# Where the operand rooms of a two-layer graph kernel lie modulo 128 bytes

## The chip, the core and the metric

The kernel runs on one core of one Trainium2 chip. The metric is the device time of one execution in microseconds. The kernel before was run three times: 1642.21, 1644.04 and 1644.42 us, so its median is 1644.04 us. One further execution was profiled: its own time was 1642.81 us, and the profile's span, from the first instruction to the last, is 1641.0 us.

Engine names below are those of the profile: PE multiplies, PEld loads the weights that a product needs, DVE is the vector engine, ACT the scalar engine, POOL the general one, and SP issues most DMAs.

## The reference, cut to what matters

Sixty-four samples of 256 rows by 512 columns go through two layers, and all samples share one 256 by 256 adjacency matrix of zeros and ones.

```
h   = relu(layernorm(x))
q, k, v = h @ Wq.T, h @ Wk.T, h @ Wv.T
rel = adj.T * (q @ k.T)
rel = rel / norm(rel, axis=2)
x   = x + rel @ v
h   = relu(layernorm(x))
x   = x + (adj @ h) @ weight + bias
```

## The kernel before, in words

**Arithmetic.** Wq and Wk are multiplied once, at the start, into one matrix `m`, so that `q @ k.T` becomes `h m h.T`. Most operands are split into three rounded parts, u, l and s ("upper", "lower" and a third one), and a product is then three sums: u by u, l by l and s by s. `three` (L329) builds such a product. The u and l sums are issued first. ACT then rescales the PSUM bank in place (L321, in `unit`), and the s sums are added behind the next unit's u and l sums.

**Tiling.** Two samples make a pair, and there are 32 pairs. For each pair PE runs six stages:

| Stage | Moving operand (right) | Loaded as weights (left) | Columns | Products |
|---|---|---|---|---|
| `g_stage` | `h_u`, `h_l`, `hs` | `m_u`, `m_l`, `m_s` | 512 | 48 |
| `v_stage` | `wv_u`, `wv_l`, `wv_s` | `h_u`, `h_l`, `hs` | 512 | 48 |
| `scores` | `h_u`, `h_l`, `hs` | `gy_u`, `gy_l`, `gy_s` | 256 | 48 |
| `attend` | `v_low`, `late_parts` | `rel_u`, `rel_l`, `rel_s_parts` | 512 | 24 |
| `gather` | `adjt_r` | `v_low`, `late_parts` | 256 | 32 |
| `mix` | `w_u`, `w_l`, `w_s` | `gy_u`, `gy_l`, `gy_s` | 512 | 48 |

All of them are issued by one line, L213. PE loads the weights of a product while the product before it streams. Layer 2 of a pair (`gather`, `mix`) runs in the middle of layer 1 of the next pair.

**Order.** `Plan` (L31) collects every operation with a cost and what it reads and writes, works out a due time for each, and emits one fixed order per engine. Every engine then works through its own list in that order and waits where an input is late.

**The work between the products.** The names that matter later, by line:

- L223, L224, L226 (`split_right_ps`): ACT writes the u part of a finished bank, DVE the s part and then the l part. For `g_stage` these are `gy_u`, `gy_s` and `gy_l`, for block columns e = 0 to 3.
- L232 to L234 (`split_left_ps`): the same for the results of `gather`.
- L250 to L260 (`norm`): DVE statistics, one square root on ACT (L256), then the reciprocal and `nb` on DVE.
- L264 (`relu`): ACT writes the normalized rows, for layer 2 into `rel_s_raw`. L477 (ACT) and L478 (DVE) split them into the parts that `gather` loads. L481 (POOL) adds the bias.
- L286 (`h_turn`): DVE transposes the next pair's rows into the rooms `h_s0` and `h_s1`, whose tiles are named `ht` and then `hs`. It has to wait until `v_stage` has read the old `hs` for the last time. L300, L302 and L295 make the three parts.
- L396 (DVE) and L400 (ACT): the masked scores and their norms. L415: 16 small DMAs on SP move the scores. L421 (DVE) transposes them, and L431 to L433 split them.
- L457 (DVE) adds the result of `attend` to x, L519 that of `mix`.

**Where the rooms lie.** `room` (L142) makes a tile in a pool with a single buffer. Rooms follow one another in the order in which they are first made, at a grain of 32 bytes per partition, and a room with a known tag reuses that tag's place. From the first room to `ident`, every size is a multiple of 128 bytes. Then come `ones`, `low_max`, `low_any`, the statistics and the norms, 928 bytes together, which is 7 times 128 plus 32. With the first room's place called 0, the program's addresses modulo 128 are:

| Place | Rooms |
|---|---|
| 0 | `m`, `wv`, `w` (all parts), `h_u`, `h_l`, `gy_u`, `gy_l` (the tags of `wq_sb`, `wk_sb`), `rel_u` (the tag of `adj_low`), `v_low` |
| 32 | `gy_s`, `rel_l`, `adjt_r`, `h_s0` and `h_s1`, `late_parts`, `rel_s` |

Offsets inside these rooms are multiples of 128 bytes throughout. So the distance, modulo 128, from a moving operand to the weights loaded while it streams is:

| Stage | u sums | l sums | s sums |
|---|---|---|---|
| `g_stage` | 0 | 0 | 96 |
| `v_stage`, `mix` | 0 | 0 | 32 |
| `scores` | 0 | 0 | 0 |
| `attend` | 0 or 96 | 0 or 32 | 0 or 32 |
| `gather` | 0, and 96 where `v_low` is loaded | | |

Where one group of sums ends and the next begins, the distance is that from the last moving operand of the one to the first weights of the other.

Of the kernel before, what the change touches and what calls it, by code (L numbers as in the profile page):

```python
# [10 lines left out]
F32R = mybir.dt.float32r  # L11
# [101 lines left out]
def kernel(  # L113
# [13 lines left out]
    B, N, D = x.shape  # L127
    DC = D // P
    NC = N // P
    NB = 2  # L130
    TC = NB * NC
    T = NB * N
# [9 lines left out]
    def room(name, *shape, dtype=F32, tag=None):  # L142
        return pool.tile([P, *shape], dtype, name=name, tag=tag or name)

    def parts_room(name, *shape, tag=None):
        return [room(f"{name}_{k}", *shape, dtype=F32R, tag=f"{tag or name}_{k}") for k in "uls"]
# [1 line left out]
    bank = [ps_m.tile([P, 512], F32, name=f"bank{n}") for n in range(8)]  # L148
    fresh = room("fresh", TC, D)
    ring = [room(f"x_ring{n}", TC, D) for n in range(2)]  # L150
    m_p, wv_p, w_p = (parts_room(w, DC, D) for w in ("m", "wv", "w"))
    h = [room(f"h_{k}", DC, T, dtype=F32R) for k in "ul"]
    ht, h_s = [None, None], [None, None]

    def hp(k, d):
        return h[k][:, d] if k < 2 else h_s[d // 2][:, d % 2]
    wq_sb, wk_sb = room("wq_sb", DC, D, tag="gy_u"), room("wk_sb", DC, D, tag="gy_l")
    adj_low = room("adj_low", 2, D, tag="rel_u")
    v_low = room("v_low", 4, D, dtype=F32R)
    blocks = room("blocks", TC, DC, P)  # L160
# [34 lines left out]
        for j in range(2)  # L195
    ]
    norms = [room(f"rn{n}", NB, NC) for n in range(2)]

    V, A, G, SP = nc.vector, nc.scalar, nc.gpsimd, nc.sync
    count = {"bank": 0}  # L200
# [38 lines left out]
    def load(plan, i, src=None, name="fresh"):  # L239

        dst = fresh if name == "fresh" else ring[i % 2]
        plan.add("SP", 0.65, lambda: SP.dma_start(out=dst, in_=xs[i]), [], keys(name, TC), lands=5.5)
# [24 lines left out]
    def h_rows(plan, i, src=fresh, name="fresh"):  # L267
        relu, needs = norm(plan, i, 0, src, name)
        for c in range(TC):
            plan.add("ACT", 0.72, lambda c=c: relu(h_rel[:, c, :], c),  # L270
                     [(name, c), *needs], [("h_rel", c)])

    def h_place(plan):
        hv = h_rel.rearrange("p c (d e) -> p c d e", e=P)

        for j in range(P // S):
            for k in range(P // S):
                plan.add("SP", 0.65, lambda j=j, k=k: SP.dma_start(  # L278
                    out=blocks[ts(j, S), :, :, ts(k, S)], in_=hv[ts(k, S), :, :, ts(j, S)]),
                    keys("h_rel", TC), [("blocks", j, k)], lands=2.3)  # L280
# [9 lines left out]
    def h_parts(plan):  # L290
        u, l = h

        def third(k, at):
            h_s[k] = room(f"hs{k}", 2, T, dtype=F32R, tag=f"h_s{k}")
            V.scalar_tensor_tensor(h_s[k], f(l[:, at]), CROSS, f(u[:, at]), op0=ALU.mult, op1=ALU.subtract)  # L295
        for k in range(2):
            d = 2 * k
            at = slice(d, d + 2)
            ku, kl, ks = ([(f"h_{q}", d), (f"h_{q}", d + 1)] for q in "uls")
            plan.add("ACT", 0.96, lambda k=k, at=at: A.activation(  # L300
                u[:, at], ht[k], AF.Copy, scale=NEAR), ks, ku)
            plan.add("DVE", 1.14, lambda k=k, at=at: V.tensor_sub(  # L302
                l[:, at], ht[k], f(u[:, at])), [*ks, *ku], kl)
            plan.add("DVE", 1.14, lambda k=k, at=at: third(k, at), [*ku, *kl], ks)
# [3 lines left out]
    def finish(plan):  # L308
        while waiting:
            waiting.pop(0)()  # L310
# [50 lines left out]
    def g_stage(plan, i):  # L361
        for e in range(DC):
            first, second = three(
                lambda k, d, e=e: m_p[k][:, d, ts(e, P)], hp,
                named("m_u", "m_l", "m_s"), h_named, MM)
            unit(plan, first, second, lambda ps, key, e=e: split_right_ps(
                plan, ps, key, [lambda at, q=q: q[:, at, :] for q in gy],
                gy_both(e), e))
# [182 lines left out]
    def before_pairs():  # L551
        A.activation(low_max, ones, AF.Sqrt)
        for _ in range(8):
            mm(bank[7][:, :P], warm, warm, True)
        V.tensor_single_scalar(low, adj_low[:, 0].bitcast(I32), 0xFFF, op=ALU.bitwise_and)
        V.tensor_reduce(low_max, low, axis=mybir.AxisListType.X, op=ALU.max)
        mm(bank[7][0:1, 0:1], low_max, ones, True)
        V.tensor_copy(low_any, bank[7][0:1, 0:1])
        for m in range(NC):
            for n in range(NC):  # L560
                nc.tensor.transpose(bank[6][:, ts(m * NC + n, P)], adj_sb[:, n, ts(m, P)], ident)
        for e in range(DC):
            for i in range(DC):
                mm(bank[i], wq_sb[:, e, ts(i, P)], wk_sb[:, e, :], e == 0)
        plan = Plan()
        h_rows(plan, 0, ring[0], "x0")
        plan.run()
        plan = Plan()
        for i in range(DC):
            split_right_ps(plan, bank[i], ("bank", i), [lambda at, q=q: q[:, at, :] for q in m_p],  # L570
                           [[("m_u", i)], [("m_l", i)], [("m_s", i)]], i)
        plan.run()

    with tc.manual_schedule(engines=in_order):
        before_pairs()
    gy = parts_room("gy", DC, T)
    rel_p = [room(f"rel_{k}", NB, NC, NC, P, dtype=F32R) for k in "ul"]
    adjt = []
    inexact = nc.values_load(low_any[0:1, 0:1], min_val=0, max_val=P * 0xFFF)
# [3 lines left out]
    def first_turn(plan):  # L583
        for d in range(DC):
            ps, key = next_bank()

            def go(ps=ps, d=d):
                for c in range(TC):
                    nc.tensor.transpose(ps[:, ts(c, P)], h_rel[:, c, ts(d, P)], ident)

            def copy(ps=ps, k=d // 2, d=d % 2):
                if not d:
                    ht[k] = room(f"ht{k}", 2, T, tag=f"h_s{k}")
                A.copy(ht[k][:, d], ps)
            plan.add("PE", 0.44, go, keys("h_rel", TC), [key])
            plan.add("ACT", 0.49, copy, [key, *([("h_s", d - 1)] if d % 2 else [])], [("h_s", d)])

    def turn_wv(plan):
        for d in range(DC):
            ps, key = next_bank()  # L600

            def go(ps=ps, d=d):
                for e in range(DC):
                    nc.tensor.transpose(ps[:, ts(e, P)], wv_sb[:, e, ts(d, P)], ident)
            plan.add("PE", 0.44, go, placed_all, [key])
            split_right_ps(plan, ps, key, [lambda at, q=q: q[:, at, :] for q in wv_p],
                           [[("wv_u", d)], [("wv_l", d)], [("wv_s", d)]], d)
# [6 lines left out]
    def pairs(exact):  # L614
        count["bank"] = 4
        waiting.clear()
        rooms.clear()
        plan = Plan()
        adjt[:] = [room("adjt_r", NC, N, dtype=F32R, tag="adjt") if exact else room("adjt", NC, N)]
        plan.add("ACT", 0.49, lambda: A.copy(adjt[0].rearrange("p m n -> p (m n)"), bank[6]), [("bank", 6)], ["adjt"])  # L620
        first_turn(plan)
        h_parts(plan)
        turn_wv(plan)
        g_stage(plan, 0)
        h_rows(plan, 1)
        h_place(plan)
        load(plan, 2)
        v_stage(plan, 0, exact, (0,))
        scores(plan, 0)
        v_stage(plan, 0, exact, (1, 2, 3))  # L630
        split_w(plan)
        finish(plan)
        turn_scores(plan, 0)
        h_turn(plan)
        h_parts(plan)
        attend(plan, 0, exact)
        for i in range(1, NP):
            load(plan, i, name=f"x{i % 2}")
            if i + 1 < NP:
                h_rows(plan, i + 1)  # L640
                h_place(plan)
            if i + 2 < NP:
                load(plan, i + 2)
            g_stage(plan, i)
            v_stage(plan, i, exact, (0,))
            v_stage(plan, i, exact, (1,), hold=True)
            scores(plan, i)
            gather(plan, i - 1, exact)
            while held:
                held.pop(0)()  # L650
            v_stage(plan, i, exact, (2, 3))
            turn_scores(plan, i)
            if i + 1 < NP:
                waiting.append(lambda: (h_turn(plan), h_parts(plan)))
                mix(plan, i - 1)
                attend(plan, i, exact)
            else:
                mix(plan, i - 1, (0, 1))
                attend(plan, i, exact)
                mix(plan, i - 1, (2, 3))  # L660
                finish(plan)
            store(plan, i - 1)
        gather(plan, NP - 1, exact)
        mix(plan, NP - 1)
        finish(plan)
        store(plan, NP - 1)
        with tc.manual_schedule(engines=in_order):
            plan.run()
# [33 lines left out]
```

## Time and profile before

| What | Value |
|---|---|
| Median of three runs | 1644.04 us |
| Profiled execution, own time | 1642.81 us |
| Its span | 1641.0 us |
| One pair in the steady middle (pairs 2 to 30) | 48.70 us |
| DVE busy in such a pair | 44.1 us |
| ACT busy in such a pair | 29.5 us |
| POOL busy in such a pair | 6.8 us |
| PE products in such a pair | 168 of 512 columns, 80 of 256 |
| First pair; last pair with the tail | 58.5 us; 77.5 us |

Times inside a pair are microseconds from the start of the span. A matmul record's duration contains a pipelined part: in this trace it is the distance to the next matmul's start plus about 163 ns. Distances between starts are therefore what PE's pace is read from, and the mean durations of two groups differ as their distances do.

### The profile page before, as it was taken

Reading aid. Unit: us, or ns where it says so; the run is one execution under the profiler, and the core shown is the slowest. Engines: PE = TensorE matmul, PEld = TensorE weight load, DVE = VectorE, ACT = ScalarE, POOL = GpSimd, SP = SyncE. Lnnn points to the kernel's source line nnn. Section 1 sums busy time; section 2 is a strip of 40 time slices with the busy share of each in tenths; the row PEclk is TensorE's granted clock in tenths of the full one; section 3 lists DMA queues with packets and bytes.
Section 4 is the critical chain, followed back from the end, with each engine's and each line's share of the span. In section 5 each row is a group of like instructions: output and inputs, shape, how many; then the busy total and the mean of one; then the engine's idle time right before and its main releaser. Section 6 shows DMA issues by size and latency. Waiting matters only on the chain.

```text
span 1641.0 us, 22555 instructions
## 1 busy us (share of the span) xinstructions
PE 1594.9 (97%) x8022; PEld 1338.1 (82%) x8022; DVE 1432.7 (87%) x2423; ACT 958.1 (58%) x1811; POOL 217.5 (13%) x168
## 2 busy tenths in 40 slices
PE   7699999999999999999999999999999999999997
PEld 4578888888888888888888888888888888888875
DVE  4789999889989889989889999888998988998874
ACT  3455656656655656565655565665665665666553
POOL 0011101111101111100111110111110111110011
PEclk9899999999999999999999999999999999999998
DMA  4324432444433343433344442344343334343111
GB/s 167 90 58 110 116 63 75 107 113 107 115 73 86 87 115 106 114 93 78 79 112 109 110 116 62 78 107 112 107 116 68 83 95 115 106 114 90 39 39 54
DMA packets 445882, 155.22 MB, mean 95 GB/s; under 512 B 402880, under 2 KB 403136, under 8 KB 445760
## 3 DMA queue, kind: packets, MB, share of 16 engines
q1 hardware_dynamic: 435264, 116.99, 30.4%
q0 software_dynamic: 8704, 33.56, 5.5%
q10 hardware_dynamic: 1792, 3.15, 0.5%
q8 instruction: 65, 1.06, 0.3%
q14 instruction: 57, 0.47, 0.1%
HBM read 70.78 MB, written 33.55 MB: 64 GB/s over the span
## 4 chain that ended last, share of the span: by engine, by line
PE 80%; DVE 9%; issue 4%; SPq 2%; ACT 2%; DMA 1%; POOL 1%; ACTq 0%; DVEq 0%; POOLq 0%
PE bank L213 80%; SPq L415 2%; DVE st L250 1%; DVE gy_l L226 1%; DVE late_parts L478 1%; DVE gy_s L224 1%; DVE hs L295 1%; SPq L278 1%; DVE x_ring L457 1%; POOL x_ring L481 0%; DVE h_l L302 0%; DMA h_rel<-h_rel 0%; DMA wk_sb<-in_L_gnn_Wk_dram 0%; ACT rel_s_raw L264 0%; DVE mv L251 0%
## 5 line engine op out<-in xcount | busy, mean ns | idle before, releaser
L321 ACT ACTIVATE bank<-bank 128x512 f32<-128x512 f32 x576 | 334.7, 581 | 429.8 <-PE bank L213 429.4
L481 POOL TENSOR_TENSOR x_ring<-x_ring,bias_bc 128x512 f32<-128x512 f32 x128 | 191.9, 1519 | 414.1 <-ACT rel_s_raw L264 414.1
L525 POOL DMA_DIRECT2D out_dram<-x_ring x32 | 24.8, 776 | 1002.1 <-DVE x_ring L519 967.1
L213 PE MATMUL bank<-h_l,m_l 128*128 128x512 f32 x512 | 139.0, 393 | 2.6 <-DVE h_l L302 2.6
L213 PE MATMUL bank<-h_u,m_u 128*128 128x512 f32 x512 | 140.2, 395 | 0.8 <-ACT h_u L300 0.8
L213 PE MATMUL bank<-w_s,gy_s 128*128 128x512 f32 x512 | 140.5, 397 | 0.0
L213 PE MATMUL bank<-w_u,gy_u 128*128 128x512 f32 x512 | 140.2, 395 | 0.0
L213 PE MATMUL bank<-wv_s,hs 128*128 128x512 f32 x512 | 139.7, 394 | 0.0
L213 PE MATMUL bank<-hs,m_s 128*128 128x512 f32 x512 | 139.6, 394 | 0.0
L213 PE MATMUL bank<-wv_u,h_u 128*128 128x512 f32 x512 | 139.3, 394 | 0.0
L213 PE MATMUL bank<-w_l,gy_l 128*128 128x512 f32 x512 | 138.7, 392 | 0.0
L213 PE MATMUL bank<-wv_l,h_l 128*128 128x512 f32 x512 | 138.0, 391 | 0.0
L213 PE MATMUL bank<-adjt_r,late_parts 128*128 128x256 f32 x896 | 127.5, 286 | 1.9 <-DVE late_parts L478 1.9
L224 DVE SCALAR_TENSOR_TENSOR gy_s<-gy_u,bank 128x512 fp32r<-128x512 f32 x128 | 86.6, 677 | 46.7 <-ACT gy_u L223 44.5
L213 PEld LDWEIGHTS bank<-adjt_r,late_parts 128*128 128x128 f32 x896 | 117.6, 193 | 2.7 <-DVE late_parts L478 2.6
L226 DVE SCALAR_TENSOR_TENSOR gy_l<-gy_s,gy_u 128x512 fp32r<-128x512 f32 x128 | 114.8, 897 | 4.3
L213 PEld LDWEIGHTS bank<-h_l,m_l 128*128 128x128 f32 x512 | 96.4, 189 | 25.0 <-DVE h_l L302 3.6
L213 PEld LDWEIGHTS bank<-h_u,m_u 128*128 128x128 f32 x512 | 96.5, 189 | 24.1 <-ACT h_u L300 1.5
L213 PEld LDWEIGHTS bank<-w_s,gy_s 128*128 128x128 f32 x512 | 96.5, 189 | 23.5 <-ACT bank L321 0.5
L213 PEld LDWEIGHTS bank<-w_u,gy_u 128*128 128x128 f32 x512 | 96.6, 189 | 22.8
L213 PEld LDWEIGHTS bank<-w_l,gy_l 128*128 128x128 f32 x512 | 96.1, 188 | 21.9
L213 PEld LDWEIGHTS bank<-hs,m_s 128*128 128x128 f32 x512 | 96.3, 188 | 21.4
(100 smaller groups left out, 3248.4 us busy)
## 6 DMA issues: line engine op xcount, KB each, us to landing
out_dram<-x_ring POOLq DMA_DIRECT2D x32, 1024.0 KB, 5.2
fresh<-in_x_dram SPq DMA_DIRECT2D x31, 1024.0 KB, 5.8
x_ring<-in_x_dram SPq DMA_DIRECT2D x31, 1024.0 KB, 8.1
blocks<-h_rel SPq DMA_DIRECT2D x496, 64.0 KB, 2.1
h_rel<-h_rel SPq DMA_DIRECT2D x512, 32.0 KB, 1.9
wq_sb<-in_L_gnn_Wq_dram SPq DMA_DIRECT2D x4, 256.0 KB, 5.0
wk_sb<-in_L_gnn_Wk_dram ACTq DMA_DIRECT2D x4, 256.0 KB, 6.1
x_ring<-in_L_gnn_weight_dram SPq DMA_DIRECT2D x1, 1024.0 KB, 13.7
```

The costliest lines, as they stand in the source:

```text
L213: nc.tensor.matmul(out, left, right, start=first, stop=True, skip_group_check=True)
L224: plan.add("DVE", 0.63, lambda: V.scalar_tensor_tensor(s(), f(u()), ONE, ps, op0=ALU.mult, op1=ALU.subtract), [*key, *ku], ks)
L226: plan.add("DVE", 0.6, lambda: V.scalar_tensor_tensor(l(), f(s()), -CROSS, f(u()), op0=ALU.mult, op1=ALU.add), [*ku, *ks], kl)
L250: V.bn_stats(st[:, c, :], src[:, c, :])
L278: plan.add("SP", 0.65, lambda j=j, k=k: SP.dma_start(out=blocks[ts(j, S), :, :, ts(k, S)], in_=hv[ts(k, S), :, :, ts(j, S)]), keys("h_rel" ...
L295: V.scalar_tensor_tensor(h_s[k], f(l[:, at]), CROSS, f(u[:, at]), op0=ALU.mult, op1=ALU.subtract)
L321: plan.add("ACT", 0.49, lambda: A.activation(ps, ps, AF.Copy, scale=ONE), [], [key])
L415: plan.add("SP", 0.65, lambda j=j, k=k: SP.dma_start(out=pv[ts(j, S), :, ts(k, S)], in_=rv[ts(k, S), :, ts(j, S)]), [("h_rel", 0), ("h_rel ...
L457: plan.add("DVE", 0.63, lambda: V.scalar_tensor_tensor(ring[slot][:, c, :], ps, rn[:, b, n : n + 1], ring[slot][:, c, :], op0=ALU.mult, op ...
L478: plan.add("DVE", 0.6, lambda c=c, u=u, l=l: V.tensor_sub(late(l), raw()[:, c % 2], f(late(u))), [*k, ("late", u)], [("late", l)])
L481: plan.add("POOL", 1.4, lambda c=c: G.tensor_tensor(ring[slot][:, c, :], ring[slot][:, c, :], bias_bc, ALU.add), [], [(f"x{slot}", c)])
L525: plan.add("POOL", 0.8, lambda: G.dma_start(out=outs[i], in_=ring[slot]), keys(f"x{slot}", TC), [], lands=6.0)
```

## The change

The order in which rooms are made is altered, and three pieces of padding are put in. Nothing that is computed differs, and no operation, cost, key or name in `Plan` does.

- The three parts of `w`, and `wq_sb` and `wk_sb` (which give `gy_u` and `gy_l` their place), are made after the small rooms, behind a pad of 32 bytes called `apart`. `gy_s` is made directly after them. A pad of 64 bytes, `apart_again`, follows.
- `adjt` gets a room that is 32 floats larger, and its data begin 16 floats, that is 64 bytes, inside it.

```
-    m_p, wv_p, w_p = (parts_room(w, DC, D) for w in ("m", "wv", "w"))
+    m_p, wv_p = (parts_room(w, DC, D) for w in ("m", "wv"))
...
-    wq_sb, wk_sb = room("wq_sb", DC, D, tag="gy_u"), room("wk_sb", DC, D, tag="gy_l")
...
     norms = [room(f"rn{n}", NB, NC) for n in range(2)]
+    room("apart", 8)
+    w_p = parts_room("w", DC, D)
+    wq_sb, wk_sb = room("wq_sb", DC, D, tag="gy_u"), room("wk_sb", DC, D, tag="gy_l")
+    gy_s = room("gy_s", DC, T, dtype=F32R)
+    room("apart_again", 16)
...
-    gy = parts_room("gy", DC, T)
+    gy = [*(room(f"gy_{k}", DC, T, dtype=F32R) for k in "ul"), gy_s]
...
-        adjt[:] = [room("adjt_r", NC, N, dtype=F32R, tag="adjt") if exact else room("adjt", NC, N)]
+        turned_adj = room("adjt_r", NC * N + 32, dtype=F32R, tag="adjt") if exact else room("adjt", NC * N + 32)
+        adjt[:] = [turned_adj[:, 16 : 16 + NC * N].rearrange("p (c n) -> p c n", c=NC)]
```

Followed through by hand, with the first room again at 0, the small rooms end at 32, `apart` brings the place to 64, the moved rooms are multiples of 128 long, and `apart_again` brings it back to 0:

| Place | Rooms after the change |
|---|---|
| 0 | `m`, `wv`, `h_u`, `h_l`, `v_low`, `rel_u`, `rel_l`, `rel_s`, `h_s0`, `h_s1`, `late_parts` |
| 64 | `w` (all parts), `gy_u`, `gy_l`, `gy_s`, the data of `adjt` |

So within every group of 512-column sums the distance becomes 0, and within every group of 256-column sums 64. Where groups of different stages meet, it is 0 or 64.

## The prediction

> **What bounds the kernel now.** I read the page's groups of instructions first. The mean duration of a 512-column product (PE lines; last number before the second bar, in ns) moves with the distance between two starts.
>
> ```profile
> L213 PE MATMUL bank<-w_s,gy_s 128*128 128x512 f32 x512 | 140.5, 397 | 0.0
> L213 PE MATMUL bank<-h_u,m_u 128*128 128x512 f32 x512 | 140.2, 395 | 0.8 <-ACT h_u L300 0.8
> L213 PE MATMUL bank<-hs,m_s 128*128 128x512 f32 x512 | 139.6, 394 | 0.0
> L213 PE MATMUL bank<-wv_l,h_l 128*128 128x512 f32 x512 | 138.0, 391 | 0.0
> L213 PE MATMUL bank<-adjt_r,late_parts 128*128 128x256 f32 x896 | 127.5, 286 | 1.9 <-DVE late_parts L478 1.9
> ```
>
> All 512-column groups do the same work, yet `w_s,gy_s` (distance 32) is 6 ns slower than `wv_l,h_l` (distance 0). `h_u,m_u` has distance 0 too and is not fast; single starts tell why. After a group at distance 96, the u and l products of `g_stage` follow one another at 231, 236, 228, 233, 231, 226, 227, 227 ns. Distance 0 settles near 226.7 ns, but only after some five products that cost 25 ns together. Distance 96 settles at 231 to 232, and distance 32 jumps between 230 and 238. Over all undisturbed 512-column products the means are 230.1 (distance 0), 233.6 (32) and 232.3 (96), 231.2 in all. 256-column products at distance 0 settle at exactly 120.0; their overall mean is 119.1.
>
> Then one steady pair as a window (busy us of each engine, then the clock), and PE's waits.
>
> ```profile
> 820.00:868.70 48.70, 48.70 (x249) 41.19 (x248) 44.18 (x76) 29.55 (x57) 6.78 (x5) 1.00 0.38 98
> ```
>
> ```profile
> PEld bank L213 <- DVE gy_l L226: 7.0, 31, 0.6
> ```
>
> The clock is at full speed, so the spacings aren't throttling. PE looks always busy, but it waits for `gy_l` in 31 places, once a pair. Its 248 products need 48.37 us of the 48.70. I number a pair's products from 0. The timeline of weight loads shows the wait, before product 84:
>
> ```profile
> 840.00 0.79 PEld L213 LDWEIGHTS bank<-h_l,gy_l 128*128 128x128 f32 x6
> 840.98 0.30 PEld L213 LDWEIGHTS bank<-h_l,gy_l 128*128 128x128 f32 x2 [0.18 <-DVE gy_l L226]
> ```
>
> A second stop of 0.10 us comes before product 122 (846.06): the s sums of `scores` wait for a rescaling on ACT that stands behind the square root of the norm, which DVE releases. From the first stop to the second, DVE and ACT work without a break, so both stops are theirs. Going back along DVE and ACT:
>
> ```profile
> 857.10 1.31 DVE L286 STREAM_TRANSPOSE ht<-blocks 128x512 f32<-128x512 f32 x2 [0.28 <-PE bank L213]
> ...
> 877.41 0.17 DVE L254 TENSOR_SCALAR rs<-mv 128x4 f32<-128x4 f32 x1
> 877.68 0.69 DVE L224 SCALAR_TENSOR_TENSOR gy_s<-gy_u,bank 128x512 fp32r<-128x512 f32 x1
> ...
> 880.80 0.69 DVE L224 SCALAR_TENSOR_TENSOR gy_s<-gy_u,bank 128x512 fp32r<-128x512 f32 x1 [1.43 <-ACT gy_u L223]
> ```
>
> ```profile
> 877.05 0.60 ACT L223 ACTIVATE gy_u<-bank 128x512 fp32r<-128x512 f32 x1 [0.40 <-PE bank L213]
> ...
> 879.47 0.81 ACT L264 ACTIVATE rel_s_raw<-x_ring,nb,rs 128x512 f32<-128x512 f32 x1
> 880.19 0.58 ACT L223 ACTIVATE gy_u<-bank 128x512 fp32r<-128x512 f32 x1
> ```
>
> The 1.43 us is not PE's either: `gy_u` for e = 1 stands on ACT behind L264, which needs DVE's `nb`. So two loops close on one pair.
>
> - Loop 1, which sets the pace: PE from product 122 to the end of the next pair's product 21 (846.06 to 876.95), then `gy_u`, and at 877.68 DVE starts the work that ends in the next stops.
> - Loop 2: PE from product 122 only to product 183, the last but two of the `hs` reads (857.06). That releases L286. DVE then works unbroken until L254.
>
> Loop 2 is early by 0.19 us: L224 starts 0.27 us after L254, but 0.077 us after it in the pair at 627 us, where a late DMA had put DVE behind. The wait is 0.19 in 22 of pairs 2 to 30 and gone in seven, where DMAs before L421 came late.
>
> **What the Trainium skill says.** "TensorE: Matmul & The Clock Gate", section "Wait — 56ns, not 53.3ns?", gives N/2.4 plus 2.5 ns between starts, 215.8 and 109.2 ns here. This trace settles at 226.7 and 120.0 at best. The same page, "Step-by-step: what each phase is for", says that the two read ports are independent and that loading the next weights takes no bandwidth from a running product. The trace contradicts that: the spacing depends on where the next weights lie. "SBUF — State Buffer", "Who interferes with whom", says that DVE with two SBUF inputs blocks while GpSimd reads SBUF. The trace agrees (L478 takes 1.79 us beside POOL's L481, 0.68 alone), and these collisions sit inside both loops. No page states a rule for places modulo 128.
>
> **The change part by part.** It removes and adds no instruction, DMA or wait, and no queue changes its order.
>
> *512-column products.* The small rooms end at 32, so the pads do what they say: every group comes to distance 0. I take 226.7 ns, and 25 ns for each restart from another distance or from 256 columns.
>
> *256-column products* come to distance 64, which the trace doesn't show. The settled values are 34 and 18 times 6.67 ns[...]. The next settled values are then 113.3 below and 126.7 above. Single products between 112 and 125 occur. I take 116.7, midway between 113.3 and today's 120.0, and keep 113 to 122, with the worse end as a rival.
>
> *DVE, ACT, POOL.* L295 reads two rooms at distance 0 in 1218 ns, and L433 two at distance 32 in 1225. So places cost DVE nothing that matters, and I cost this at nothing. If wrong by 7 ns on each of the thirty or so SBUF-to-SBUF operations of loop 2, that is 0.2 us a pair either way.
>
> *PE in loop 2* (products 122 to 183): 32 products of 256 columns took 3.82 us without the stop and become 3.73; 29 of 512 took 6.71 and become 6.57 plus 0.06 for restarts. Saved: 0.16 us.
>
> *PE in loop 1*: the same and 86 more of 512 columns, 19.89 us, which become 19.50 plus six restarts, 19.65. Saved in all: 0.40 us.
>
> Loop 1 would then take 48.30, loop 2 48.70 - 0.19 - 0.16 = 48.35. Loop 2 becomes the longer: a pair saves 0.35 us, and the rest of PE's gain goes into longer stops before product 84. What is late next is DVE. The chain of SP's 16 DMAs isn't: the last landed 1.05 us before L421 in a normal pair, and 0.16 us of this is used up.
>
> *Sum.* 22 pairs by 0.35 are 7.7 us. In the seven disturbed pairs loop 2 has no slack to give, so they save 0.16, 1.1 together. For the first two pairs and the end, where PE runs ahead only in parts, I estimate 0.4 (about half a pair's gain of PE alone). Together 9.2 us: a span of 1631.8 and an own time of 1633.6. The profiled execution was 1.2 us below the median, so I put 1634.8 for the median.
>
> **Rivals.**
> - PE alone sets the time. For it: PE 97% busy. Then 168 products by about 3.2 ns (4.5 less restarts) and 80 by 2.4 give 0.73 us a pair, 22 us: 1622. Against it: PE already stops twice a pair, behind DVE and ACT.
> - The spacing doesn't settle, and 512 columns merely get today's mean at distance 0, 230.1, with 256 columns unchanged. Loop 1 saves 115 by 1.1, 0.13 us, about 3.7 in all: 1640.3. For it: `h_u,m_u` lies at 0 and is slow. Against it: what comes before it explains this.
> - Slower: 256 columns at distance 64 settle between 126.7 and 133.3, say 130. The place is the stretch before product 122, 34 such products with only 0.10 us of cover: 0.37 - 0.02 - 0.10 = 0.25 us. Loop 2's own 32 cost 0.35, less 0.07 and 0.19: 0.09. Together 0.34 a pair, 10 us: 1654. It decides from about 125 ns a product. For it: 32 and 96 are worse than 0 with 512 columns. Against it: distances 32 and 96 gave 118.0 and 119.9 with 256.
>
> **How the numbers follow.** The forecast gets 0.68, PE alone 0.10, no settling 0.13, slower 0.09. With 256 columns at 113.3, loop 2 saves 0.46 and the time is 1631.7; with 122 it is 1639.6. The range 1628 to 1642 covers these with the DVE doubt and the second rival; PE alone and slower, 0.19, stay outside. Faster by over 0.2% (3.3 us, about what a measurement of this kernel can tell from no change): 0.66 of the forecast, all of PE alone, half of the second rival, 0.82. Within 0.2%: 0.02, 0.07 and 0.01 of the third, 0.10. Slower: 0.08.
>
> **What would show it.** All 512-column groups should have mean durations of 389 to 391 ns, and those with an s part lose most. The wait for `gy_l` before product 84 should grow from 0.18 to some 0.45 us. L224 should follow L254 by 0.08 us in ordinary pairs, and a pair should take 48.35 us. I am wrong if DVE's unbroken stretch from L286 to L254 changes its length, if a pair falls below 48.2 us, or if 256 columns stand above 125 ns.

## The result and the profile after

The changed kernel took 1631.78 us (median of four runs, 1631.09 to 1633.35). The kernel before took 1643.4 us beside it (four runs, 1642.21 to 1644.42). The ratio is 0.9931, with a 95% interval of 0.9914 to 0.9948: faster by 11.6 us. The profiled execution of the changed kernel took 1631.09 us and its span is 1629.3 us, against 1642.81 and 1641.0. Lines of the changed kernel from `room` on stand 7 further down (L213 is L220, L254 is L261, and so on).

I start with the page's groups of the changed kernel, the five whose like the prediction shows (last number before the second bar: mean ns of one).

```profile
L220 PE MATMUL bank<-hs,m_s 128*128 128x512 f32 x512 | 139.2, 393 | 0.0
L220 PE MATMUL bank<-h_u,m_u 128*128 128x512 f32 x512 | 139.0, 393 | 0.8 <-ACT h_u L307 0.8
L220 PE MATMUL bank<-w_s,gy_s 128*128 128x512 f32 x512 | 138.0, 392 | 0.0
L220 PE MATMUL bank<-wv_l,h_l 128*128 128x512 f32 x512 | 137.4, 390 | 0.0
L220 PE MATMUL bank<-adjt_r,late_parts 128*128 128x256 f32 x896 | 125.0, 282 | 1.5 <-DVE late_parts L485 1.5
```

`w_s,gy_s` fell from 397 to 392 and the 256-column group from 286 to 282. `hs,m_s` moved by 1 ns only, though its distance went from 96 to 0 modulo 128. Over all undisturbed products of pairs 2 to 29 the distance between starts fell from 231.2 to 229.2 ns (512 columns) and from 119.1 to 117.8 (256 columns).

Now one steady pair as a window, and the wait for `gy_l` among PE's waits (us in total, times, longest).

```profile
1110.20:1158.57 48.37, 48.34 (x249) 41.13 (x248) 44.05 (x77) 29.69 (x57) 6.77 (x5) 1.00 0.40 98
```

```profile
PEld bank L220 <- DVE gy_l L233: 10.5, 31, 0.8
```

A pair takes 48.37 us, where it took 48.70. PE's saving isn't all used: the wait for `gy_l` rose from 7.0 to 10.5 us in total, still once a pair. The timeline of weight loads in that pair shows the stop before product 84, 0.23 us where it was 0.18:

```profile
1127.13 0.78 PEld L220 LDWEIGHTS bank<-h_l,gy_l 128*128 128x128 f32 x6
1128.14 0.30 PEld L220 LDWEIGHTS bank<-h_l,gy_l 128*128 128x128 f32 x2 [0.23 <-DVE gy_l L233]
```

And the timeline of DVE, from the transpose that ends loop 2's part on PE to the start of the next pair's `gy_s`:

```profile
1144.15 1.30 DVE L293 STREAM_TRANSPOSE ht<-blocks 128x512 f32<-128x512 f32 x2 [0.24 <-PE bank L220]
...
1164.45 0.17 DVE L261 TENSOR_SCALAR rs<-mv 128x4 f32<-128x4 f32 x1
1164.53 0.68 DVE L231 SCALAR_TENSOR_TENSOR gy_s<-gy_u,bank 128x512 fp32r<-128x512 f32 x1
```

DVE's stretch from L293 to L261 is 20.30 us long, and was 20.31 (857.10 to 877.41): the places of the rooms cost DVE nothing. L231 now starts 0.08 us after L261, and it did so in all pairs. The 0.19 us by which loop 2 was early are gone. Loop 1 ends with `gy_u` on ACT:

```profile
1163.89 0.60 ACT L230 ACTIVATE gy_u<-bank 128x512 fp32r<-128x512 f32 x1 [0.40 <-PE bank L220]
```

It ended at 1164.49 us. Over pairs 2 to 30 L231 started 0.036 us (median) after that end, where before, when loop 1 alone set the pace, it had been 0.032. So in the changed kernel the two loops are level within 4 ns. This trace alone can't say which one sets the pace; the run `hs_at_256` below can.

By stretches of a pair (medians of pairs 2 to 29, from the starts of the products in the trace, us), with two of the experiments beside them:

| Products | Columns | Before | After | `all_at_zero` | `hs_at_256` |
|---|---|---|---|---|---|
| 0 to 22 | 512 | 5.073 | 5.029 | 5.099 | 4.987 |
| 22 to 64 | 512 | 9.685 | 9.635 | 9.735 | 9.520 |
| 64 to 84, with the first stop | both | 3.192 | 3.244 | 3.145 | 3.480 |
| 84 to 122 | mostly 256 | 5.075 | 5.073 | 5.084 | 5.073 |
| 122 to 154, with the rest of the second stop | 256 | 3.919 | 3.866 | 3.898 | 3.878 |
| 154 to 183 | 512 | 6.708 | 6.637 | 6.643 | 6.614 |
| 183 to 228 | 512 | 10.422 | 10.259 | 10.227 | 10.226 |
| 228 to 248 | 512 | 4.627 | 4.624 | 4.608 | 4.575 |
| Median pair | | 48.70 | 48.37 | 48.45 | 48.35 |

And the span of each profiled execution in four parts (us). `before_bias_later` and `after_bias_later` are experiments below, whose edit had no effect: their engines work off the same operations in the same order as the kernel before and the changed one.

| Part of the span | Before | `before_bias_later` | After | `after_bias_later` |
|---|---|---|---|---|
| To the start of pair 1 | 91.90 | 93.81 | 91.80 | 91.69 |
| Pair 1 | 48.36 | 48.36 | 48.02 | 47.87 |
| Pairs 2 to 30 | 1413.55 | 1414.06 | 1405.64 | 1405.44 |
| Last pair and the tail | 87.15 | 83.80 | 83.84 | 84.09 |

The steady pairs give 7.9 us and pair 1 gives 0.34. The last part seems to give 3.3 us more. The windows of that part in these three traces, of before, of `before_bias_later` and of after, show the granted clock as the third number from the end:

```profile
1553.81:1640.97 87.16, 71.58 (x331) 58.32 (x329) 54.21 (x87) 35.11 (x67) 14.18 (x11) 0.89 0.18 56
```

```profile
1556.24:1640.00 83.76, 68.76 (x331) 56.21 (x329) 54.02 (x87) 35.13 (x67) 14.16 (x11) 0.93 0.18 58
```

```profile
1545.46:1629.29 83.83, 68.16 (x331) 56.28 (x329) 54.14 (x87) 35.14 (x67) 14.14 (x11) 0.93 0.19 58
```

The rooms of the kernel before gave 87.16 us at a clock of 0.89 and 83.76 at 0.93. So the 3.3 us aren't shown to be the change's. What is before pair 1 varies too, by 1.9 us with the old rooms. (The 77.5 us in the table of before count only to the start of the last product; to the end of the span it is 87.15.)

### The profile page after: what moved, and what is told of

Same layout as the page of the kernel before. It is cut to its first block, busy times and chain, and to the rows that moved or that the text cites. A ratio compares the mean times of both kernels' runs of the same rounds, so it can differ in the third digit from the quotient of the medians.

```text
span 1629.3 us, 22555 instructions
## 1 busy us (share of the span) xinstructions
PE 1580.3 (97%) x8022; PEld 1333.4 (82%) x8022; DVE 1430.1 (88%) x2423; ACT 958.5 (59%) x1811; POOL 217.5 (13%) x168
## 4 chain that ended last, share of the span: by engine, by line
PE 71%; DVE 14%; SPq 6%; ACT 3%; issue 3%; DMA 2%; POOL 0%; ACTq 0%; DVEq 0%; POOLq 0%
PE bank L220 71%; SPq L422 5%; DVE gy_l L233 2%; DVE st L257 2%; DVE late_parts L485 2%; DVE gy_s L231 1%; DVE hs L302 1%; DVE x_ring L464 1%; DMA h_rel<-h_rel 1%; DVE h_l L309 1%; SPq L285 1%; DVE rel_l L439 1%; DVE x_ring L526 1%; ACT rel_u L438 1%; ACT h_rel L271 1%
## 5 line engine op out<-in xcount | busy, mean ns | idle before, releaser
L220 PE MATMUL bank<-h_l,m_l 128*128 128x512 f32 x512 | 138.5, 392 | 2.5 <-DVE h_l L309 2.5
L220 PE MATMUL bank<-wv_s,hs 128*128 128x512 f32 x512 | 140.1, 395 | 0.0
L220 PE MATMUL bank<-h_u,m_u 128*128 128x512 f32 x512 | 139.0, 393 | 0.8 <-ACT h_u L307 0.8
L220 PE MATMUL bank<-hs,m_s 128*128 128x512 f32 x512 | 139.2, 393 | 0.0
L220 PE MATMUL bank<-wv_u,h_u 128*128 128x512 f32 x512 | 138.2, 391 | 0.0
L220 PE MATMUL bank<-w_s,gy_s 128*128 128x512 f32 x512 | 138.0, 392 | 0.0
L220 PE MATMUL bank<-w_u,gy_u 128*128 128x512 f32 x512 | 137.8, 391 | 0.0
L220 PE MATMUL bank<-wv_l,h_l 128*128 128x512 f32 x512 | 137.4, 390 | 0.0
L220 PE MATMUL bank<-w_l,gy_l 128*128 128x512 f32 x512 | 136.8, 389 | 0.0
L220 PE MATMUL bank<-adjt_r,late_parts 128*128 128x256 f32 x896 | 125.0, 282 | 1.5 <-DVE late_parts L485 1.5
L231 DVE SCALAR_TENSOR_TENSOR gy_s<-gy_u,bank 128x512 fp32r<-128x512 f32 x128 | 86.5, 676 | 44.4 <-ACT gy_u L230 44.4
L233 DVE SCALAR_TENSOR_TENSOR gy_l<-gy_s,gy_u 128x512 fp32r<-128x512 f32 x128 | 114.8, 897 | 4.3
L220 PEld LDWEIGHTS bank<-adjt_r,late_parts 128*128 128x128 f32 x896 | 116.1, 191 | 2.0 <-DVE late_parts L485 1.9
L220 PEld LDWEIGHTS bank<-h_u,m_u 128*128 128x128 f32 x512 | 96.7, 189 | 23.6 <-ACT h_u L307 1.5
L220 PEld LDWEIGHTS bank<-h_l,m_l 128*128 128x128 f32 x512 | 96.4, 189 | 23.9 <-DVE h_l L309 3.6
L220 PEld LDWEIGHTS bank<-w_s,gy_s 128*128 128x128 f32 x512 | 96.4, 189 | 21.8 <-ACT bank L328 1.2
L220 PEld LDWEIGHTS bank<-w_u,gy_u 128*128 128x128 f32 x512 | 96.1, 188 | 21.2
L220 PEld LDWEIGHTS bank<-hs,m_s 128*128 128x128 f32 x512 | 96.0, 188 | 20.8
L220 PEld LDWEIGHTS bank<-wv_l,h_l 128*128 128x128 f32 x512 | 96.1, 188 | 20.4
```

The costliest lines, as they stand in the source:

```text
L220: nc.tensor.matmul(out, left, right, start=first, stop=True, skip_group_check=True)
L231: plan.add("DVE", 0.63, lambda: V.scalar_tensor_tensor(s(), f(u()), ONE, ps, op0=ALU.mult, op1=ALU.subtract), [*key, *ku], ks)
L233: plan.add("DVE", 0.6, lambda: V.scalar_tensor_tensor(l(), f(s()), -CROSS, f(u()), op0=ALU.mult, op1=ALU.add), [*ku, *ks], kl)
```

## The experiments

### The spacing by itself

`spacing_by_distance` has none of the reference's computation. It issues products by PE alone from two rooms, 24 in a row at each distance between the moving operand and the weights that are loaded while it streams. The offsets within the rooms step by 2048 bytes, as in:

```
+            a = at // 4 + j * 512
+            w = (at + dist) // 4 + j * 512
...
+                bank[count // 8 % 8][:, :cols], left[:, w : w + 128], right[:, a : a + cols],
...
```

> PE alone, nothing of the reference computed: runs of 24 products each at one distance from the moving operand to the next weights, for 512 and 256 columns, distances 0 to 224 bytes in steps of 32 and some longer, from three places of the moving operand. Theory A (the period is 128 bytes): distance 128 settles like 0 (226.7 ns with 512 columns) and 192 like 64 (about 117.7 with 256 columns). Theory B (the period is 256 bytes, which would explain why the hs groups of the changed kernel, at 128 modulo 256, alternate 234, 224, 238, 229): distance 128 settles near 231 with 512 columns, and 256 like 0. Theory C (the distance doesn't matter, the DVE and ACT traffic of the kernel makes the differences): all distances show one spacing.

Measured from the starts in its trace: means in ns of the last 16 distances of each run of 24, good to some 0.3 ns where the values repeat in threes or sixes. From every place of the moving operand that was tried they came out the same, within 0.1 ns over the last 11 distances (0, 64 and 128; 0 and 128 for the last two columns):

| Distance in bytes | 0 | 32 | 64 | 96 | 128 | 160 | 192 | 224 | 384, 640 | 256, 512, 1024 |
|---|---|---|---|---|---|---|---|---|---|---|
| 512 columns | 226.7 | 233.3 | 233.3 | 234.2 | 233.3 | 233.6 | 228.9 | 233.3 | 232.9 | 226.7 |
| 256 columns | 120.0 | 118.3 | 117.75 | 117.2 | 118.6 | 119.9 | 117.75 | 117.9 | 118.6 | 120.0 |

The period is 256 bytes and not 128: 256, 512 and 1024 behave as 0, while 384 and 640 come within 0.5 ns of 128. At 128 a 512-column product costs 6.6 ns more than at 0. With 256 columns the distance 64 is 2.25 ns better than 0.

That bears on the change. By the program's addresses `adjt`'s new room is 2176 bytes long, an odd multiple of 128, so everything made after it (`hs`, `late_parts`, `rel_s`) lies 128 bytes off `m`, `wv` and `h` modulo 256. In the changed kernel those are the groups that didn't settle: `hs,m_s` jumps through 234, 224, 238 (mean within its groups 231.9) and `wv_s,hs` has a mean of 233.0, while `w_l,gy_l` and `wv_l,h_l` stand at 226.7 and 226.8.

### What the distance of 64 is worth

`all_at_zero` puts the 256-column products back to a distance of 0 modulo 128.

```
-    room("apart", 8)
+    room("apart", 24)
...
-    room("apart_again", 16)
...
-        adjt[:] = [turned_adj[:, 16 : 16 + NC * N].rearrange("p (c n) -> p c n", c=NC)]
+        adjt[:] = [turned_adj[:, : NC * N].rearrange("p (c n) -> p c n", c=NC)]
```

> The changed kernel with w, gy and the data of adjt at place 0 as well, so 512-column groups keep distance 0 modulo 128 and 256-column groups have it too. If the 512-column products bring the gain: they keep about 229.2 ns on average, 256 columns rise from 117.7 to about 119.5, 32 of them lie in loop 2, so a pair takes 48.37 + 0.06 = 48.43 us and the run about 2 us more than the changed kernel. If the distance of 64 with 256 columns brings the gain: a pair goes back to 48.6 or more, 8 us more.

It took 1636.68 us (seven runs, 1633.88 to 1639.64), a ratio to the kernel before of 0.9963 (0.9951 to 0.9975). A pair took 48.45 us, near the 48.43 expected. The run took 4.9 us more than the changed kernel where 2 had been expected; of the 3.5 us between the two profiled spans, pairs 2 to 30 give 2.0 and the time before pair 1 gives 1.3. The mean distance between 256-column starts went back to 119.1 ns. So of the 0.33 us that the change brings in a pair, 0.25 stay without the distance of 64; they come from the places of the 512-column operands.

The other 0.08 us isn't the distance of 64 alone. In ordinary pairs of `all_at_zero` `gy_s` starts 0.033 us after `gy_u` again and 0.09 instead of 0.08 after the line before it, so loop 1 sets the pace there. PE's stretch of loop 2, products 122 to 183, lost only 0.04 us by the table. In loop 1, products 0 to 22 took 0.07 us more, and that isn't distance: products 0 to 64 have the same distances modulo 256 in both kernels, and each kernel shows both values. They took 14.83 us in the steady pairs of `all_at_zero` and in pair 1 of the changed kernel, and 14.66 us in pair 1 of `all_at_zero` and in the steady pairs of the changed kernel. How much of the 0.08 is due to the distance stays open.

### One product more, inside and outside the loops

A 512-column product is issued twice, and its second issue overwrites the first: in `one_more_late` in the block c = 2 of `v_stage`, which lies inside both loops, in `one_more_early` in the block c = 0, which lies between the end of loop 1's part (product 21) and the first stop.

```
+            if c == 2:
+                def first(ps, usual=first, c=c):
...
+                        mm(ps, hp(0, 0)[:, ts(c, P)], wv_p[0][:, 0, :], True)
```

> The changed kernel with one product of 512 columns issued twice in each pair, the first of v_stage's third block (product 126, inside PE's stretch of loop 2; its result is overwritten). Loops theory: all of its 0.23 us comes on top, a pair takes 48.60 us, the run 7 us more. PE alone sets the pace: the same, 48.60.

> The changed kernel with one product of 512 columns issued twice in each pair, the first of v_stage's first block (product 46, before the first stop, outside loop 2; its result is overwritten). Loops theory: the first stop has 0.19 us of idle to give, so a pair takes 48.37 to 48.42 us, the run 0 to 2 us more, and the idle before product 84 shrinks to near nothing. PE alone sets the pace: a pair takes 48.60 us and the run 7 us more.

`one_more_late`: pair 48.587, so 0.220 us more, and 1638.67 us in one run. `one_more_early`: the median pair stayed at 48.367, and its one run took 1636.08 us, over the 0 to 2 us more that were expected. Where a whole product is added without lengthening a pair, PE's sum can't be what sets the pair. PE's waits of `one_more_early` show where it went:

```profile
PEld bank L220 <- DVE gy_l L233: 5.2, 12, 0.6
```

The wait for `gy_l` is left in 12 places instead of 31: the product filled the stop. The 4 us that the whole run lost against the changed kernel aren't in the median pair: of pairs 2 to 30, 12 were over 0.03 us longer than it, where 9 had been. Pairs in which DVE came late to L231 (`gy_u` lay ready for over 0.1 us) became more, 10 against 8, by a cause that I didn't follow.

### hs, late_parts and rel_s moved on by 128 bytes

```
-        turned_adj = room("adjt_r", NC * N + 32, dtype=F32R, tag="adjt") if exact else room("adjt", NC * N + 32)
+        turned_adj = room("adjt_r", NC * N + 64, dtype=F32R, tag="adjt") if exact else room("adjt", NC * N + 64)
```

> The changed kernel with adjt's room 32 floats longer, so that hs, late_parts and rel_s move up by 128 bytes and every group of 512-column sums is at distance 0 modulo 256; 256-column groups are at 64 or 192, which settle alike. Period of 256 bytes: hs and late_parts groups settle at 226.7 as w_s,gy_s did, all 512-column products average some 227.3 instead of 229.2. Loops theory: only six such products lie in PE's stretch of loop 2, so a pair takes 48.32 to 48.34 us against 48.37, the run 1 us less, and the first stop grows by some 0.25 us. PE alone sets the pace: a pair falls by 0.32 to 48.05, the run by 10 us. Period of 128 bytes: nothing changes.

The time was 1632.81 us (four runs, 1631.96 to 1635.24), ratio 0.9942 (0.9924 to 0.9959). A pair took 48.35, just over the 48.32 to 48.34 expected. This is the purest of the runs: PE became faster by 0.37 us in the pair without stops, and the time didn't move. Its group of `hs,m_s`:

```profile
L220 PE MATMUL bank<-hs,m_s 128*128 128x512 f32 x512 | 136.8, 389 | 0.0
```

and its wait for `gy_l`:

```profile
PEld bank L220 <- DVE gy_l L233: 19.6, 31, 1.0
```

`hs,m_s` settles at 226.7 ns, the mean over all 512-column products is 227.4. Pair 1, which has no stops, fell to 47.647 us (48.362 before, 48.021 after the change). In the other pairs most of this went into the stop before product 84, whose total rose from 10.5 to 19.6 us. Products 122 to 183 took 10.49 us against 10.50, and with DVE's stretch unchanged that is all that loop 2 could give. This run also tells the two loops apart:

```profile
1116.69 0.60 ACT L230 ACTIVATE gy_u<-bank 128x512 fp32r<-128x512 f32 x1 [0.38 <-PE bank L220]
```

```profile
1117.38 0.17 DVE L261 TENSOR_SCALAR rs<-mv 128x4 f32<-128x4 f32 x1
1117.46 0.68 DVE L231 SCALAR_TENSOR_TENSOR gy_s<-gy_u,bank 128x512 fp32r<-128x512 f32 x1
```

`gy_u` now ended 0.16 us before L231 (median 0.160, against 0.036), so loop 1 had become early by some 0.12 us, and L231 still followed L261 by 0.08. The pair lost 0.014 us. Loop 2 sets the pace.

### The additions of the bias taken out of DVE's way: first try

The two loops predict that DVE is worth shortening. In the stretch that both loops share, behind L231, DVE has two long operations beside GpSimd's additions (L485 of 1.78 us and L233 of 1.54, where the same operations take 0.68 and 0.69 when GpSimd is quiet). So I gave these additions (`add_bias`) a later place in `Plan`, with the split of v into `v_low` as something that they read.

```
-                ring[slot][:, c, :], ring[slot][:, c, :], bias_bc, ALU.add), [], [(f"x{slot}", c)])
+                ring[slot][:, c, :], ring[slot][:, c, :], bias_bc, ALU.add), behind, [(f"x{slot}", c)])
...
+            add_bias(plan, i - 1, [("late", 1)])
```

> The kernel before with POOL's four bias additions of a pair put behind the next pair's v_low split instead of beside L478 and L226, where they held DVE up for about 1.1 and 0.85 us in both loops. Loops theory: both loops get about 1.9 us shorter, PE then has no stop before products 84 and 122 and sets the pace: a pair takes 48.36 us (what the one pair without stops took) against 48.70, the run about 10 us less than before. If DVE doesn't set the pace: 48.70 stays.

> The same move of POOL's additions in the changed kernel. Loops theory: no stops, PE sets the pace, a pair takes 48.02 us (what the changed kernel's one pair without stops took) against 48.37, the run about 10 us less than the changed kernel, some 1621 us. If DVE doesn't set the pace: 48.37 stays.

> The changed kernel with hs, late_parts and rel_s at distance 0 modulo 256 and POOL's additions later. Loops theory: with PE setting the pace all of its gain counts: a pair takes about 47.70 us, the run some 1611 us. If the hs rooms' place didn't matter: as with the later additions alone, about 1621 us.

Nothing moved. 1642.68 us (ratio 1.0001, 0.9992 to 1.001), 1631.63 (0.9936, 0.9919 to 0.9954) and 1633.0 (0.9937, 0.9919 to 0.9955), with pairs of 48.71, 48.37 and 48.35 us: the kernel before, the changed one and `hs_at_256` over again. GpSimd started where it had started, because a key in `Plan` orders the list of an engine but isn't a wait: nothing that the additions read was written by the split. These three runs test nothing of the theory. They are repeats, and were used as such above.

### The same with a real wait

Now GpSimd first copies one column of the next pair's `v_low` into a small room, and the additions stand behind that copy.

```
+        def look():
...
+            G.tensor_copy(gate[0], f(late(1))[:, :1])
+        if behind:
+            plan.add("POOL", 0.1, look, behind, ["gate"])
...
+                ring[slot][:, c, :], ring[slot][:, c, :], bias_bc, ALU.add), ["gate"], [(f"x{slot}", c)])
```

> The kernel before, and GpSimd reads one column of the next pair's v_low ahead of the four additions of bias_bc, so that they really wait behind VectorE's split of v into v_low and run where VectorE has no operation with two operands in SBUF. The rooms are the kernel before's. Two-loops theory: the slow stretches of VectorE in which it and GpSimd add at the same time (1.1 us more on h, 0.85 us more on late, by the durations of the same operations where GpSimd is quiet) leave both of VectorE's stretches, TensorE alone sets the pace: pair 48.36 us against 48.70, no stop before products 84 and 122, run about 10 us below the kernel before. If VectorE sets no pace: pair 48.70, run 1642 to 1643.

> The changed kernel with the same wait of GpSimd's additions. Two-loops theory: the stops before products 84 and 122 go, and what is left is the sum of TensorE's spacings with the new rooms: pair about 48.02 us against 48.37, run about 1621. If VectorE sets no pace: pair 48.37, run 1631 to 1632.

> The changed kernel with hs, late and rel_s moved on by 128 bytes and the same wait of GpSimd's additions. Two-loops theory: pair 47.65 us (what pair 1 took without stops in the run with hs moved alone), run 1609 to 1611. If VectorE sets no pace: pair 48.35, run 1632 to 1633.

In `before_bias_waits` DVE's timeline has the short forms,

```profile
1173.05 0.69 DVE L478 TENSOR_TENSOR late_parts<-rel_s_raw,v_low 128x512 fp32r<-128x512 f32 x1
...
1175.28 0.69 DVE L226 SCALAR_TENSOR_TENSOR gy_l<-gy_s,gy_u 128x512 fp32r<-128x512 f32 x1
```

and GpSimd's timeline has all four additions in a row, after the split:

```profile
1181.55 0.18 POOL L489 COPY gate<-v_low 128x1 f32<-128x1 f32 x1 [18.05 <-DVE v_low L226]
1181.69 5.03 POOL L493 TENSOR_TENSOR x_ring<-x_ring,bias_bc 128x512 f32<-128x512 f32 x4
```

The Trainium skill, "SBUF — State Buffer", section "Who interferes with whom", says that a DVE instruction with two SBUF inputs contends with a GpSimd instruction that reads SBUF. These runs agree: with the additions gone from beside it, L478 takes 0.69 us instead of 1.79.

| | Pair expected | Pairs without a stop | How many of pairs 2 to 30 | Run expected | Run measured | Ratio to before |
|---|---|---|---|---|---|---|
| `before_bias_waits` | 48.36 | 48.366 | 14 | some 10 us less | 1638.02 | 0.9976 (0.9968 to 0.9984) |
| `after_bias_waits` | 48.02 | 47.873 | 9 | 1621 | 1629.0 | 0.9911 (0.989 to 0.9933) |
| `both_wait` | 47.65 | 47.646 | 1 (and pair 1) | 1609 to 1611 | 1626.47 | 0.9904 (0.9886 to 0.9922) |

The pairs without a stop came where the theory had put them, in two of three kernels within 0.01 us. With old rooms and no stop a pair is PE's own sum, 48.37; so both stops were DVE's and GpSimd's, and neither loop is left in those pairs. In `after_bias_waits` such pairs are 0.15 us shorter than expected. The 48.02 had been taken from pair 1 of the changed kernel, whose products 0 to 64 ran in the slower of their two ways, 14.83 us; in these nine pairs they took 14.66. From about product 133 the 256-column products ran at 113, 113, 114 ns in pair 1 of the changed kernel, in all of these nine pairs and in five of the other pairs from 2 to 30; in the rest, as in pairs 2 to 29 of the changed kernel, they stood at 117.75.

The runs gained far less than these pairs, for the other pairs had a stop again, before product 122 and up to 1.1 us long. DVE's group of the statistics on `fresh`, the x that is read for a later pair, is the place. In the changed kernel it had no idle time before it:

```profile
L257 DVE BATCH_NORM_STATS2 st<-fresh 128x6 f32<-128x512 f32 x124 | 83.3, 671 | 0.0
```

and in `both_wait` it has, by its group and by the timeline of one pair:

```profile
L257 DVE BATCH_NORM_STATS2 st<-fresh 128x6 f32<-128x512 f32 x124 | 83.6, 674 | 13.5 <-DMA fresh<-in_x_dram 13.1
```

```profile
1361.39 0.69 DVE L233 SCALAR_TENSOR_TENSOR gy_l<-gy_s,gy_u 128x512 fp32r<-128x512 f32 x1
1362.92 0.69 DVE L257 BATCH_NORM_STATS2 st<-fresh 128x6 f32<-128x512 f32 x1 [0.84 <-DMA fresh<-in_x_dram]
```

SyncE asks for this read behind 16 transfers of `blocks`, 7.2 to 9.0 us into a pair (pairs 2 to 29 of `both_wait`), and it lands at 12.8 to 14.9. In the changed kernel DVE comes to it at 14.86, so it was in time. In `both_wait` DVE could begin at 13.28, and in the waiting pairs began about 0.02 us after the landing.

But the late read is only half of the cause. L261, which follows these statistics and releases the square root ahead of product 122, now runs beside GpSimd's additions. It reads one small tensor, took 0.17 us in the changed kernel, and takes 1.18 to 1.21 us in 27 of pairs 2 to 29 of `both_wait`. The pair of the timeline above, pair 27, is one of them:

```profile
1370.11 1.19 DVE L261 TENSOR_SCALAR rs<-mv 128x4 f32<-128x4 f32 x1
```

The one exception is pair 7. DVE waited there for the read just as long, but the additions began 0.35 us later in the pair, and L261 was soon past:

```profile
396.84 0.70 DVE L257 BATCH_NORM_STATS2 st<-fresh 128x6 f32<-128x512 f32 x1 [0.84 <-DMA fresh<-in_x_dram]
...
404.03 0.30 DVE L261 TENSOR_SCALAR rs<-mv 128x4 f32<-128x4 f32 x1
```

Pair 7 took 47.753 us and pair 27 took 48.667. In both other kernels of this section pair 7 has a late read and a short L261 too, and no stop. So the new stops come from the late read and the additions' new place together. An estimate, with everything else held as it was: taking from each stop before product 122 in pairs 2 to 29 of `both_wait` what L261 took over 0.17 us leaves 0.9 us of 18. The run would then be near 1609 us, where it was expected. No run tried it.

### The read of x asked for first

```
                 h_rows(plan, i + 1)
-                h_place(plan)
             if i + 2 < NP:
                 load(plan, i + 2)
+            if i + 1 < NP:
+                h_place(plan)
```

> The kernel of both_wait, and SyncE issues the read of x two pairs on (fresh) ahead of the 16 transfers of blocks instead of behind them. In both_wait that read landed 12.8 to 14.9 us into a pair, and VectorE, which now came to its statistics (L257) at 13.28, waited for it in most pairs. Theory (the landing of fresh took the place of the two loops): it lands some 10 us earlier, the stops before product 122 shrink to the 0.1 us of the pairs in which it landed early, pair 47.73 us in nearly all, run about 1610 (28 pairs took 17.5 us more than 47.73 each; some 2 us of that come from the score transfers and stay). If the stop before product 122 has another cause: pair 48.3, run 1626.

This took 1628.34 us (four runs, 1625.24 to 1629.95), ratio 0.9906 (0.9882 to 0.993), and the order on SyncE was the old one: `Plan` picks the most urgent of what is ready, and the 16 transfers are more urgent. The read was asked for at 7.2 to 9.1 us as before. So it is a second run of `both_wait`, and what an earlier read would bring is open. The two profiled spans, 1625.0 and 1625.8 us, lie below the changed kernel's two, 1629.3 and 1629.1. So moving `hs` and the additions together is some 4 us faster than the change alone, though the intervals of the two ratios overlap.

## Why the prediction was right, and where it wasn't

The forecast was 1634.8 us and faster; the median was 1631.78. It had put the saving at 9.2 us. Of the 11.6 measured, pairs 1 to 30 give 8.2, so the mechanism accounts for the pairs, and that the whole came so near owes something to parts that nothing here explains. Its steps in turn:

- **Loop 2 takes over, and a pair takes 48.35 us.** Right: 48.367, L231 follows L261 by 0.08 us in every pair, DVE's stretch is unchanged. The runs with one product more show that only what lies inside the loops lengthens a pair, `hs_at_256` shows that it is loop 2 and not loop 1, and the runs with the real wait show DVE and GpSimd as the cause of both stops.
- **All 512-column groups come to distance 0 and to 389 to 391 ns.** Wrong for the groups with `hs` and parts of `attend`. The step that failed is the period of 128 bytes; it is 256. PE alone was to gain 0.73 us a pair and gained 0.34 by pair 1 of the changed kernel, or 0.49 by pair 1 of `after_bias_later`, which has the same rooms (48.02 and 47.87 in the table of parts). In `hs_at_256`, with that put right, it gains 0.715. That this is so near 0.73 is luck in part: starts with 512 columns fell by 3.8 ns where 3.2 had been put in, and those with 256 by 1.4 where 2.4 had been.
- **Loop 1 saves 0.40, loop 2 0.16.** By the stretches 0.33 and 0.12. Loop 1 alone would then stand at 48.70 - 0.33 = 48.37, level with loop 2; the forecast had put it 0.05 below. The two errors hardly touched the pair, since loop 2 sets it; but it sets it by so little that a slightly smaller gain in loop 1, as in `all_at_zero`, gives the pace back to loop 1. That was luck too.
- **The stop before product 84 grows to 0.45 us.** It grew to 0.23. The term that was mis-sized is PE's gain outside loop 2, for the reason above; `hs_at_256` has 0.51.
- **256-column products at 116.7 ns.** 117.75 settled, inside the bounds of 113 and 122. 117.75 isn't a multiple of 6.67 ns, so the rule by which the prediction had worked out the next settled values doesn't hold. The value of 113.3 exists all the same, in pairs of `after_bias_waits`. (The 0.46 us that the prediction gives loop 2 with 113.3 is what a pair would save; loop 2 itself would save 0.27, and the rest is its slack of 0.19.)
- **22 ordinary pairs by 0.35 and seven disturbed by 0.16, 8.8 us in all.** The trace gives 7.9. Over their ordinary lengths, pairs 2 to 30 lost 1.25 us before (1413.55 - 29 x 48.70) and 3.0 after (1405.64 - 29 x 48.367). The slack of 0.19 that had covered late transfers is gone, and they cost more than I took.
- **First pairs and the end, 0.4 us.** The profiles show 3.8 us for pair 1, the start and the end together. Most is the end under a lower clock, which differed as much between two runs with the old rooms. How much of it is the change's stays open, and so does why the medians differ by 11.6 us where pairs 1 to 30 give 8.2.

Of the rivals, PE alone falls with `one_more_early` and `hs_at_256`. No settling falls with the groups at 226.7 ns. Slower needed 256 columns above 125 ns, and no distance gave more than 120.0.

## What to carry to other kernels

Before a gain on one engine is priced, follow the waits around the whole loop and ask which stretches of that engine lie inside the loop that sets the pace: PE gained 0.72 us a pair in `hs_at_256` and the pair 0.35, as much as the loop through DVE allowed. When a loop is shortened, look for the transfer that was in time by little, here 0.3 us in its latest pair. When work is moved out of the way of one operation, look in the new trace for the operation that it now holds up, here L261, 1.19 us for 0.17. And look in the new trace whether an edit of a planned order moved anything at all before its time is read.

## What the runs showed of the hardware that was not expected

- The distance between starts of products depends on where the weights that are loaded meanwhile lie, relative to the moving operand, modulo 256 bytes: 226.7 to 234.2 ns with 512 columns, 117.2 to 120.0 with 256. The Trainium skill, "TensorE: Matmul & The Clock Gate", section "Step-by-step: what each phase is for", has the two reads independent; these runs contradict it.
- One distance can have more than one settled state. 256-column products at a distance of 64 modulo 128 stood at 117.75 ns in most pairs and at 113.3 in all pairs of `after_bias_waits` that no stop had broken and in a few others. Products 0 to 22 took 5.03 or 5.10 us with the same rooms, in the steady pairs and in pair 1 of the changed kernel. What chooses the state was not tried.
- A small DVE operation with one tensor as its input can be held up beside GpSimd too: L261 (128 by 4) took 1.18 to 1.21 us in 27 of pairs 2 to 29 of `both_wait`, and 0.17 in the changed kernel.
- The last pair and the tail took 83.8 or 87.2 us with the same rooms and the same order, with a mean clock of 0.93 or 0.89 there.
